# Mask loads and first-maxima loads begun by GpSimd, query loads spread over steps, and chains begun later, in a two-layer attention kernel

## The chip, the cores and the metric

The kernel runs on one core of a Trainium2 chip. The metric is the device time of one execution in microseconds. A core has five engines with a queue each: TensorE (PE in the profile; PEld are its weight loads), VectorE (DVE), ScalarE (ACT), GpSimd (POOL) and SyncE (SP), which only begins transfers here. An engine takes its instructions in the order of the program and waits at each for the semaphores that this instruction needs, so a waiting instruction holds all behind it.

## The reference

Two transformer layers work on x (2048 rows of 256) with 16 heads of 16.

```
layer 0: x0, x1 = halves of x (1024 rows each)
         each half: x += gate * self_attention(mod(ln(x)))
         xm, ym = mod(ln(x0)), mod(ln(x1));  x0 attends to ym, x1 attends to xm, gated
         x += gate * mlp(mod(ln(x)))          # 256 -> 1024 -> 256, gelu
layer 1: x = ln(x + attention(x, x, mask))    # scores = where(mask == 0, -1e9, scores)
         x = ln(x + attention(x, ctx))        # ctx: 1601 rows
         x = ln(x + mlp(x))                   # relu
attention: softmax(q k^T / 4) v, per head, then an output projection
```

The mask is a 2048 x 2048 array of int32. All is float32.

## The kernel before

**Stages, blocks, units, steps.** There are four attention stages: 0 self, 1 cross, 2 masked, 3 over the context. A stage goes over four blocks of 512 queries, a block over four groups of four heads. One group of one block is a unit. In stages 0 and 1 a unit has 16 steps, in stage 2 it has 32, in stage 3 it has 26. Block 2 of stage 2 goes first and is split into two parts by keys, so that its first part (4 units of 16 steps) needs only half the keys; the parts are joined at the end. This makes 1440 steps; one takes about 1.9 us.

**A step** does two things on TensorE. It makes one tile of scores of the current unit by key rows (L1160; in stage 2 the mask's bias is first added by L1153), adds the negated row maximum (L1167), takes the exponential on ScalarE (L1174), and adds an earlier tile's product with the values to the sums (L1191). And it makes one tile of scores of the *next* unit by query rows (L1079, and L1074 in stage 2), only for its maxima, which VectorE takes (L1089; in stage 2 L1082, which adds the bias by rows first). When a unit's maxima are complete they are negated and turned into a row tile `nm` (L1113, copied by ScalarE at L1118), three steps later. Both kinds of score tile share three PSUM buffers.

**Split block.** For its eight units the first maxima are needed in another layout too: `as_rows` begins eight small loads `mh<-nm` (L1125) and four steps later VectorE adds them (L1131, `minus`).

**End of a unit.** At step 2 of the next unit, `copy_sums` copies the sums (L1223) and moves them by 4 + 4 transfers (L1229, L1238) to `weights` and `oT`. Three steps later the weights are inverted and go through memory to `rd_rows` (L1260, L1262); six steps later GpSimd divides oT by them (L1269).

**Chains.** What follows attention for a block is a generator of the background: the projection (L544), a gate on GpSimd (`gated`, L563 and L565, which finish the tile `t`), normalization (statistics on VectorE, the power `rs` on GpSimd at L387, then L390), transposes (L405), in stages 1 and 3 the feed-forward layer (L602, L655; in stage 1 with a gate), then keys, queries (L454) and values (L490) of the next stage. Keys and queries are split into a high and a low part, `hi` (ScalarE, L467) and `lo` (VectorE, L468), in a ring of three buffers, and stored by SP (L472). Values go to a tile `v` that GpSimd first sets to one in part (L483). A chain is advanced by a step at a time, one piece of TensorE work each. `chain_after` sets when it may begin: 8 steps after `copy_sums`, or 9 for the split block.

**Order.** The program's order on every queue is what this planning writes out; nothing reorders it later. `later` holds actions with a countdown in steps; `after` runs those due, then one key or value transfer of the next stage, then advances the chain. A chain leaves out a step in which such an action, like the turn of nm, uses TensorE.

**Loads on SP.** `load_queries` (L981) begins the eight transfers of a unit's queries at step 1, two units ahead, into one of three buffers. `mask_rows` loads a 128 x 512 tile of the mask into one of two buffers `raw` (L1014), and GpSimd makes a bias tile of it (L1015). There are 64 such tiles: 8 for each part of the split block, one a step (`mask_part`), and 16 for each other block, begun among the maxima of the last unit of the block before. All transfers are begun by SP.

Of the kernel before, what the change touches and what calls it, by code (L numbers as in the profile page):

```python
# [12 lines left out]
F32 = mybir.dt.float32  # L13
# [9 lines left out]
P = 128  # L23
D = 256
H = 16
HD = 16
# [4 lines left out]
BLK = 512  # L31
# [45 lines left out]
def two_layers(ctx: ExitStack, tc: tile.TileContext, a: dict, out: bass.AP):  # L77
    nc = tc.nc
# [875 lines left out]
    def load_needed(kind, u):  # L954

        need = [(kind, u["st"], u["g"], slot) for slot in u["slots"]]
        load_ready(need)
        assert all(w in loaded for w in need)
# [11 lines left out]
        elif transfers:  # L970
            transfers.pop(0)[1]()

    def load_queries(u):
        st, b, g = u["st"], u["b"], u["g"]
        ensure(("q", st, b))
        u["q"] = sb.tile([P, 2, BLK], F32R, tag="q", bufs=3, name="q")
        d = queries_dr[st, b]
        for c in range(2):
            for i in range(4):
                at = 64 * c + HD * i  # L980
                nc.sync.dma_start(  # L981
                    u["q"][at : at + HD].bitcast(F32),
                    d[c, i // 2, 2 * g * HD : (2 * g + 2) * HD, :].rearrange(
                        "(q d) t -> d q t", d=HD
                    ),
                )

# [6 lines left out]
    def mask_rows(b, slot, qt, j):  # L996

        if (b, slot, qt) not in bias_rows:
            if b != SPLIT:
                t = sb.tile([P, 2, SLOT], BF16, tag="w_mlp", bufs=WB, name="bias")  # L1000
                for s in range(2):
                    bias_rows[b, s, qt] = t[:, s, :]
            elif slot == 0:

                t = sb.tile([P, TPB, SLOT], BF16, tag="kT11", name="bias")
                for q in range(TPB):
                    bias_rows[b, slot, q] = t[:, q, :]
            else:
                t = sb.tile([P, 2, SLOT], BF16, tag="w_mlp", bufs=WB, name="bias")
                for q2 in range(2):  # L1010
                    bias_rows[b, slot, qt + q2] = t[:, q2, :]
        raw = sb.tile([P, BLK], I32, tag="raw", bufs=2, name="raw")
        q0, k0 = b * BLK + qt * P, KEYS[2][slot][j] * BLK
        nc.sync.dma_start(raw, a["mask"][q0 : q0 + P, k0 : k0 + BLK])  # L1014
        nc.gpsimd.tensor_scalar(  # L1015
            bias_rows[b, slot, qt][:, j * BLK : (j + 1) * BLK], raw, 0.0, MASKED,
            ALU.is_equal, ALU.mult,
        )
# [26 lines left out]
    def maxima(u):  # L1045

        st, b, g = u["st"], u["b"], u["g"]
        masked = st == 2
        chunks = []
        for slot in u["slots"]:  # L1050
            nk = slot_rows(st, slot)
            n = -(-nk // BLK)
            size = -(-nk // n)
            size += size % 2
            nk += nk % 2
            chunks += [(slot, c, min(size, nk - c)) for c in range(0, nk, size)]

        def pair(qt, n, i):
            if "pm" not in u:
                load_needed("keys", u)  # L1060
                u["pm"] = sb.tile([P, TPB, 2, 2, len(chunks)], F32, tag="pm", bufs=2, name="pm")
            if masked and i == 0 and g == NG - 1 and 1 in u["slots"]:
                at = ORDER[2].index(b) + 1
                each = 2 * 2 // len(chunks)
                for j in range(n * each, (n + 1) * each) if at < NB else ():
                    mask_rows(ORDER[2][at], j // 2, qt, j % 2)
            slot, c, nn = chunks[n]
            s = big_ps()
            for h in range(2):
                queries = u["q"][64 * h : 64 * h + 64, i, qt * P : (qt + 1) * P]  # L1070
                keys = kT[g][slot][64 * h : 64 * h + 64, i, c : c + nn]
                if masked and h:
                    for part in range(2):
                        nc.tensor.matmul(  # L1074
                            exchanged(s[:, h, :], part), lhsT=queries,
                            rhs=exchanged(keys, 1 - part), start=True, stop=True,
                        )
                    continue
                nc.tensor.matmul(s[:, h, :nn], lhsT=queries, rhs=keys, start=True, stop=True)  # L1079
            if masked:  # L1080
                for h in range(2):
                    nc.vector.tensor_tensor_reduce(  # L1082
                        out=s[:, h, :], in0=s[:, h, :],
                        in1=bias_rows[b, slot, qt][:, c : c + nn],
                        scale=1.0, scalar=-3.0e38, op0=ALU.add, op1=ALU.max,
                        accum_out=u["pm"][:, qt, h, i, n : n + 1],
                    )
            else:
                nc.vector.tensor_reduce(u["pm"][:, qt, :, i, n], s[:, :, :nn], AX.X, ALU.max)  # L1089

        return [
            lambda qt=qt, n=n, i=i: pair(qt, n, i)
            for qt in range(TPB) for n in range(len(chunks)) for i in range(2)
        ]
# [14 lines left out]
    def as_rows(u):  # L1109

        m = one_ps()
        for qt in range(TPB):
            nc.tensor.matmul(  # L1113
                m[:, qt * P : (qt + 1) * P], lhsT=negpad[:, qt, :], rhs=identR,
                start=True, stop=True,
            )
        u["nm"] = sb.tile([P, BLK], F32R, tag="nm", bufs=2, name="nm")
        nc.scalar.copy(u["nm"], m)  # L1118
        if "part" in u:

            t = sb.tile([P, 2, 4 * BLK // P], F32, tag="mh", bufs=2, name="mh")
            for j in range(4):
                for h in range(2):
                    r = 64 * (j // 2) + 2 * (j % 2) + h
                    nc.sync.dma_start(  # L1125
                        t[PH * j : PH * (j + 1), h, :], u["nm"][r : r + 1, :].bitcast(F32)
                    )

            def add():
                n = u["minus"] = part_tile(u, "minus")  # L1130
                nc.vector.tensor_tensor(n, t[:, 0, :], t[:, 1, :], ALU.add)  # L1131

            later.append([4, add, False])
# [189 lines left out]
            nc.vector.reciprocal(rd[rows_, cut], rd[rows_, cut])  # L1323
            nc.vector.tensor_tensor(oT[:, cut], oT[:, cut], rd[rows_, cut], ALU.mult)

    def chain_after(u):

        go = now[0] + (9 if "part" in u else 8)

        def gen():  # L1330
            yield max(0, go - now[0])
            yield from chains[u["st"]](u["b"])

        background.append([gen(), 0, False])

    def stream(stages):
# [78 lines left out]
        streaming[0] = True  # L1415
        for u in units[:2]:
            load_queries(u)
        for step in range(math.floor(todo[-1][0]), 0):
            small[0] = 1
            evict()  # L1420
            take_maxima(step)
            after(step)
        pending: list = []
        step = 0
        for u in units:
            i = u["i"]
            masked = u["st"] == 2
            small[0] = i % 2
            second = weights_of(u)
            for s2 in range(len(second)):  # L1430
                if masked:
                    evict()
                if s2 == 3:
                    pending += values_of(u)
                if s2 == 1 and i + 2 < len(units):
                    load_queries(units[i + 2])

                if masked:
                    second[s2]()
                take_maxima(step)  # L1440
                f = pending.pop(0) if pending else None


                after(step)
                if f:
                    f()
                if not masked:

                    evict()
                    second[s2]()  # L1450
                step += 1
                if s2 == 2:
                    small[0] = (i + 1) % 2
                if s2 == 2 and i:
                    w = units[i - 1]
                    copy_sums(w)
                    part = w.get("part")
                    if part is None:
                        later.append([3, lambda w=w: invert(w), False])
                        later.append([6, lambda w=w: divide(w), False])  # L1460
                    elif part == 1:
                        v = units[i - 1 - NG]
                        later.append([3, lambda w=w, v=v: compare(w, v), False])
                        later.append([4, lambda w=w, v=v: invert_both(w, v), False])
                        later.append([7, lambda w=w: (fetch_first(w), divide(w)), False])
                    if w["g"] == NG - 1 and part != 0:
                        chain_after(w)
        small[0] = len(units) % 2
        last_t.append(residual(xs[3, units[-1]["b"]]))
        for f in pending:  # L1470
# [120 lines left out]
```

## Time and profile before

| | us |
|---|---|
| median of 3 runs | 3239.06 |
| the runs | 3213.37, 3239.06, 3241.68 |
| profiled execution, whole time | 3233.97 |
| its span in the trace | 3232.2 |
| TensorE busy | 2965.8 |
| VectorE busy | 2174.8 |
| ScalarE busy | 1718.1 |
| GpSimd busy | 389.5 |

The mean granted clock of TensorE is 0.97 of full. In the profile "A <- B" reads: A stood idle until B released it. "raw<-in_mask" names a transfer by what it writes and reads. In a timeline the columns are start, duration, engine, line, operation, tiles, shapes and count; a bracket tells the idle time before, and who ended it. In a table of windows each engine's busy time in the stretch is followed by its number of instructions; then come the granted clock, the share of time in which the DMA engines were busy, and GB/s.

By the trace, stage 0 and the unmasked part of stage 1 last until about 1199 us, the split block from 1199 to about 1640, the other masked blocks until about 2350, stage 3 to the end.

### The profile page before, as it was taken

Reading aid. Unit: us, or ns where it says so; the run is one execution under the profiler, and the core shown is the slowest. Engines: PE = TensorE matmul, PEld = TensorE weight load, DVE = VectorE, ACT = ScalarE, POOL = GpSimd, SP = SyncE. Lnnn points to the kernel's source line nnn. Section 1 sums busy time; section 2 is a strip of 40 time slices with the busy share of each in tenths; the row PEclk is TensorE's granted clock in tenths of the full one; section 3 lists DMA queues with packets and bytes.
Section 4 is the critical chain, followed back from the end, with each engine's and each line's share of the span. In section 5 each row is a group of like instructions: output and inputs, shape, how many; then the busy total and the mean of one; then the engine's idle time right before and its main releaser. Section 6 shows DMA issues by size and latency. Waiting matters only on the chain.

```text
span 3232.2 us, 60041 instructions
## 1 busy us (share of the span) xinstructions
PE 2965.8 (92%) x24128; PEld 1449.1 (45%) x24128; DVE 2174.8 (67%) x3945; ACT 1718.1 (53%) x1897; POOL 389.5 (12%) x333
## 2 busy tenths in 40 slices
PE   5899999999999889998999999999989999999997
PEld 2344444444444345444555555554444444444443
DVE  4676776767565647566878878877667757657452
ACT  1465655656464536443555555555556546546462
POOL 0001101101010121204013013110010110110110
PEclk8899999999999999998999999999999999999998
DMA  6462162162114321254111011003240000000000
GB/s 165 129 132 87 51 110 67 46 125 41 60 27 94 60 84 40 90 104 125 45 49 57 18 34 60 21 26 77 44 105 19 21 17 21 26 19 28 11 14 18
DMA packets 177155, 191.39 MB, mean 59 GB/s; under 512 B 94036, under 2 KB 110940, under 8 KB 176876
## 3 DMA queue, kind: packets, MB, share of 16 engines
q1 hardware_dynamic: 176876, 187.55, 23.6%
q8 instruction: 190, 3.11, 0.4%
q14 instruction: 89, 0.73, 0.1%
HBM read 129.78 MB, written 48.45 MB: 55 GB/s over the span
## 4 chain that ended last, share of the span: by engine, by line
PE 74%; DVE 7%; ACT 6%; DMA 6%; SPq 3%; issue 2%; POOL 1%; ACTq 0%; DVEq 0%; POOLq 0%
PE m_ps L1191 20%; PE s_ps L1160 16%; PE s_ps L1167 8%; PE s_ps L1079 7%; ACT e L1174 5%; PE s_ps L1153 5%; PE m_ps L602 3%; PE m_ps L655 3%; PE m_ps L454 2%; PE m_ps L490 2%; PE m_ps L544 2%; DVE s_ps L1082 2%; DMA kT<-k_dr 2%; DVE pm L1089 2%; PE s_ps L1074 2%
## 5 line engine op out<-in xcount | busy, mean ns | idle before, releaser
L1174 ACT ACTIVATE e<-s_ps 128x1024 f32<-128x1024 f32 (+1 forms) x1440 | 1466.4, 1024 | 1200.1 <-PE s_ps L1167 1180.8
L1089 DVE TENSOR_REDUCE pm<-s_ps 128x2 f32<-128x1024 f32 (+3 forms) x1024 | 1121.6, 1107 | 499.8 <-PE s_ps L1079 496.4
L1191 PE MATMUL m_ps<-e,V 128*32 128x256 f32 (+2 forms) x10432 | 910.6, 421 | 0.9 <-DVE lo L468 0.8
L1082 DVE CUSTOM_DVE_ANT_0 s_ps<-s_ps,bias 128x512 f32<-128x512 f32 x1024 | 712.7, 701 | 216.0 <-PE s_ps L1074 193.4
L1160 PE MATMUL s_ps<-q,kT 64*128 64x512 f32 (+1 forms) x2880 | 721.7, 498 | 28.8 <-ACT e L1174 23.3
L1079 PE MATMUL s_ps<-kT,q 64*128 64x512 f32 (+3 forms) x2560 | 602.0, 394 | 103.1 <-ACT e L1174 66.2
L1167 PE MATMUL s_ps<-nm,sel 64*128 64x512 f32 (+1 forms) x2880 | 574.2, 395 | 0.0
L1160 PEld LDWEIGHTS s_ps<-q,kT 64*128 64x128 f32 (+1 forms) x2880 | 270.0, 184 | 568.4 <-issue 404.4
L1079 PEld LDWEIGHTS s_ps<-kT,q 64*128 64x128 f32 x2560 | 293.1, 187 | 273.7 <-ACT e L1174 151.6
L1191 PEld LDWEIGHTS m_ps<-e,V 128*32 128x32 f32 (+1 forms) x10432 | 207.3, 109 | 348.5 <-issue 285.1
L1269 POOL TENSOR_TENSOR oT<-oT,rd_rows 64x512 f32<-64x512 f32 x63 | 80.2, 1273 | 1793.3 <-DMA rd_rows<-rd_dr 1419.8
L1167 PEld LDWEIGHTS s_ps<-nm,sel 64*128 64x128 f32 (+1 forms) x2880 | 276.1, 188 | 2.0
L1153 PE MATMUL s_ps<-biasT,ident 64*64 64x512 bf16 x2048 | 210.7, 402 | 9.0 <-DVE pm L1082 6.2
L1074 PE MATMUL s_ps<-kT,q 64*128 64x256 f32 x1024 | 206.0, 282 | 10.8 <-DMA kT<-k_dr 10.0
L1074 PEld LDWEIGHTS s_ps<-kT,q 64*128 64x128 f32 x1024 | 184.1, 185 | 33.6 <-issue 10.8
L1153 PEld LDWEIGHTS <-ident 64*64 64x64 bf16 x2048 | 58.3, 103 | 231.0 <-issue 164.4
L1015 POOL TENSOR_SCALAR bias<-raw 128x512 bf16<-128x512 int32 x64 | 123.6, 1931 | 247.8 <-DMA raw<-in_mask 233.0
L1082 DVE DVE_READ_ACCUMULATOR2_ANT pm<- 128x1 f32 x1024 | 144.8, 141 | 0.0
L454 PE MATMUL m_ps<-hT,w_qk 128*128 128x512 f32 (+2 forms) x224 | 111.9, 623 | 10.7 <-DVE lo L468 7.7
L602 PE MATMUL m_ps<-hT,w_mlp 128*128 128x512 f32 x224 | 111.1, 618 | 5.9 <-ACT sums L1223 4.4
L468 DVE SCALAR_TENSOR_TENSOR lo<-m_ps,qkb,hi 128x512 fp32r<-128x512 f32 (+3 forms) x60 | 42.0, 700 | 108.5 <-ACT hi L467 64.7
L655 PE MATMUL m_ps<-w_mlp,hid 128*128 128x256 f32 x448 | 105.0, 388 | 0.0
(118 smaller groups left out, 1414.9 us busy)
## 6 DMA issues: line engine op xcount, KB each, us to landing
q<-q_dr SPq DMA_DIRECT2D x544, 64.0 KB
kT<-k_dr SPq DMA_DIRECT2D x192, 128.0 KB
raw<-in_mask SPq DMA_DIRECT2D x64, 256.0 KB
q_dr<-hi SPq DMA_DIRECT2D x32, 256.0 KB
q_dr<-lo SPq DMA_DIRECT2D x32, 256.0 KB
oT<-sums SPq DMA_DIRECT2D x256, 32.0 KB
rd_rows<-rd_dr SPq DMA_DIRECT2D x63, 128.0 KB
k_dr<-hi SPq DMA_DIRECT2D x28, 256.0 KB
```

The source lines that it names most:

```text
L454: nc.tensor.matmul(m[:, :n], lhsT=wqk[:, k, w, c, :], rhs=hT[:, k, :n], start=k == 0, stop=k == 1)
L602: nc.tensor.matmul(m, lhsT=w1[k][:, f * P : (f + 1) * P], rhs=hT[:, k, :], start=k == 0, stop=k == 1,)
L655: nc.tensor.matmul(m[:, q2 * D : (q2 + 1) * D], lhsT=hid[f][:, qt * P : (qt + 1) * P], rhs=w2[f // 4][:, f % 4, :], start=f == 0, stop=f = ...
L1074: nc.tensor.matmul(exchanged(s[:, h, :], part), lhsT=queries, rhs=exchanged(keys, 1 - part), start=True, stop=True,)
L1079: nc.tensor.matmul(s[:, h, :nn], lhsT=queries, rhs=keys, start=True, stop=True)
L1082: nc.vector.tensor_tensor_reduce(out=s[:, h, :], in0=s[:, h, :], in1=bias_rows[b, slot, qt][:, c : c + nn], scale=1.0, scalar=-3.0e38, op0 ...
L1089: nc.vector.tensor_reduce(u["pm"][:, qt, :, i, n], s[:, :, :nn], AX.X, ALU.max)
L1153: nc.tensor.matmul(s[to : to + 64, h, :], lhsT=ident16[of : of + 64, of : of + 64], rhs=bias_columns[b, slot, kt][of : of + 64, :], start= ...
L1160: nc.tensor.matmul(s[:r, h, :], lhsT=kT[g][slot][64 * h : 64 * h + 64, i, kt * P : kt * P + r], rhs=u["q"][64 * h : 64 * h + 64, i, :], st ...
L1167: nc.tensor.matmul(s[:r, h, :], lhsT=sel[64 * h : 64 * h + 64, i, :r], rhs=u["nm"][64 * h : 64 * h + 64, :], start=False, stop=True,)
L1174: nc.scalar.activation(e[:r], s[:r], AF.Exp, scale=SCALE)
L1191: nc.tensor.matmul(u["av"][PH * j : PH * (j + 1), cut], lhsT=V[g][slot][:r, kt * GW + j * VW : kt * GW + j * VW + PH], rhs=u["e"][n, j % 2 ...
```

## The change

Four edits, in three parts.

1. `mask_rows` begins the load of raw on GpSimd's queue instead of SP's. In GpSimd's order each load then stands directly ahead of the instruction that makes the bias of it.
2. `as_rows` begins the eight loads mh on GpSimd's queue.
3. `load_queries` only allots the buffer and makes a list of eight loads. For the first two units all are issued at once; otherwise one is issued a step, and what is left is issued before the unit's maxima begin.
4. `chain_after` lets a chain begin 11 steps after `copy_sums` instead of 8, unless the current stage is the masked one. Together with the turn of nm at step 13 of a unit, the projection then stands at steps 14 and 15 of a 16-step unit (before: 10 and 11), in stage 3 at 13 and 14 (before: 10 and 11), and all that the chain does comes three or four steps later. In stage 2 the order on TensorE is the same as before.

```diff
-    def load_queries(u):
+    def load_queries(u, spread=False):
         st, b, g = u["st"], u["b"], u["g"]
         ensure(("q", st, b))
         u["q"] = sb.tile([P, 2, BLK], F32R, tag="q", bufs=3, name="q")
         d = queries_dr[st, b]
...
+        def load(c, i):
+            at = 64 * c + HD * i
+            nc.sync.dma_start(
+                u["q"][at : at + HD].bitcast(F32),
+                d[c, i // 2, 2 * g * HD : (2 * g + 2) * HD, :].rearrange("(q d) t -> d q t", d=HD),
+            )
+
+        u["loads"] = [lambda n=n: load(n // 4, n % 4) for n in range(8)]
+        if spread:
+            for n in range(8):
+                later.append([n, lambda: u["loads"] and u["loads"].pop(0)(), False])
...
-        nc.sync.dma_start(raw, a["mask"][q0 : q0 + P, k0 : k0 + BLK])
+        nc.gpsimd.dma_start(raw, a["mask"][q0 : q0 + P, k0 : k0 + BLK])
         nc.gpsimd.tensor_scalar(
             bias_rows[b, slot, qt][:, j * BLK : (j + 1) * BLK], raw, 0.0, MASKED,
...
             if "pm" not in u:
+                while u["loads"]:
+                    u["loads"].pop(0)()
                 load_needed("keys", u)
...
-                    nc.sync.dma_start(
+                    nc.gpsimd.dma_start(
                         t[PH * j : PH * (j + 1), h, :], u["nm"][r : r + 1, :].bitcast(F32)
                     )
...
-    def chain_after(u):
+    def chain_after(u, masked=False):
...
-        go = now[0] + (9 if "part" in u else 8)
+        go = now[0] + (9 if "part" in u else 8 if masked else 11)
...
             load_queries(u)
+            while u["loads"]:
+                u["loads"].pop(0)()
...
-                    load_queries(units[i + 2])
+                    load_queries(units[i + 2], spread=True)
...
-                        chain_after(w)
+                        chain_after(w, masked)
```

More of the change, by code (lines that the diff above doesn't have):

```diff
@@ L977, in load_queries @@
         d = queries_dr[st, b]
-        for c in range(2):
-            for i in range(4):
-                at = 64 * c + HD * i
-                nc.sync.dma_start(
[L982 to L986, printed above, removed]
+        def load(c, i):
[8 more added lines that the diff above has]
+                later.append([n, lambda: u["loads"] and u["loads"].pop(0)(), False])
     bias_rows: dict = {}
@@ L1124, in as_rows @@
                     r = 64 * (j // 2) + 2 * (j % 2) + h
-                    nc.sync.dma_start(
+                    nc.gpsimd.dma_start(
                         t[PH * j : PH * (j + 1), h, :], u["nm"][r : r + 1, :].bitcast(F32)
```

## The prediction

> **What bounds the kernel now.** I read the page's busy shares and clock row first, then the waits, then the stretches where TensorE (PE) idles, then the queues there.
>
> ```profile
> PE 2965.8 (92%) x24128; PEld 1449.1 (45%) x24128; DVE 2174.8 (67%) x3945; ACT 1718.1 (53%) x1897; POOL 389.5 (12%) x333
> PEclk8899999999999999998999999999999999999998
> ```
>
> PE is busy 92%, 2966 of 3232 us. Only the other 266 us, and what a lowered clock costs, can be won by moving transfers. The windows show that little of it is general:
>
> ```profile
> 1050.00:1100.00 50.00, 38.02 (x286) 17.81 (x279) 29.50 (x40) 23.50 (x26) 7.35 (x6) 0.93 0.55 92
> 1150.00:1200.00 50.00, 37.87 (x240) 19.53 (x239) 22.30 (x37) 18.12 (x22) 19.45 (x12) 0.86 0.34 112
> 1350.00:1400.00 50.00, 40.67 (x327) 19.44 (x319) 25.12 (x68) 18.90 (x21) 0.00 (x0) 0.90 0.54 101
> 1500.00:1550.00 50.00, 39.45 (x290) 20.38 (x288) 30.08 (x88) 16.54 (x21) 23.97 (x14) 0.86 0.34 109
> 1700.00:1750.00 50.00, 50.00 (x512) 25.51 (x513) 41.59 (x113) 28.97 (x30) 4.63 (x3) 1.00 0.11 31
> ```
>
> The columns are PE, PEld, DVE, ACT, POOL busy, then the granted clock. The steady masked stage (1700) has no hole. Around the start of that stage single holes of 6 to 11 us stand, and each drags the clock down: 0.86 over 50 us is 7 us of full clock, beside 11.2 us of standing. PE's waits name them:
>
> ```profile
> PE m_ps L490 <- DVE lo L468: 28.9, 8, 11.2
> PE m_ps L544 <- POOL oT L1269: 11.8, 3, 6.1
> PE s_ps L1074 <- DMA kT<-k_dr: 10.0, 2, 7.8
> PE m_ps L405 <- ACT sums L1223: 10.0, 7, 1.4
> PE m_ps L454 <- DVE lo L468: 7.7, 14, 1.7
> ```
>
> (total, times, longest). The longest L490 wait is explained by SP's queue at that moment:
>
> ```profile
> 1161.96 7.59 SPq L1014 DMA_DIRECT2D raw<-in_mask  x4
> ...
> 1173.09 0.38 SPq L472 DMA_DIRECT2D k_dr<-hi  x1
> ```
>
> Four mask loads, each waiting until GpSimd (POOL) has used up one of two raw buffers, stand ahead of the store of hi. DVE waits 11.9 us for that store to free its tile, and PE waits for DVE.
>
> **What is won.** (1) With raw off SP, that 11.2 us stall goes. (2) The 7.8 us wait for keys at 1375: SP held the last three key loads behind eight mh loads (issued 1365.48 to 1370.5, after a wait for nm). Without them the loads go some 5 us earlier; I leave 1.5 us, so 6.3. (3) Projections start at step 14 of a unit, not step 10 (11 instead of 8, and the turn of nm at step 13 pushes them on): four steps of 1.9 us (64 steps lie between the projections at 249.3 and 371.6) outlast L544's waits of 1.5, 6.1 and 4.2, so 11.8. (4) The same shift takes four 1.4 us waits of L405 behind ACT's sums away, 5.7 us, and lets hi and lo be stored after the weights and oT copies of step 2 are issued (389.60 to 395.8 on SP): 5 of L454's 7.7 us. The shift's loads of x and its residual go with it and were never waited for. Its PE work is the same rows, 0. Long stalls: 29.3; short ones: 10.7.
>
> The stalls at 1484 and 1531 (3.1 and 7.4 us, again L490 behind lo) have the same cause as (1), but I don't count them: there POOL becomes late instead, below.
>
> **What it costs.** 64 mask loads and 64 mh loads (first maxima) move onto POOL: in its order each raw load now stands directly ahead of its own bias (L1015), so load and use cannot overlap any more. Before, SP ran ahead by two buffers:
>
> ```profile
> 1321.49 1.92 POOL L1015 TENSOR_SCALAR bias<-raw 128x512 bf16<-128x512 int32 x1 [0.97 <-DMA raw<-in_mask]
> 1323.49 1.27 POOL L563 TENSOR_TENSOR u<-u,rows 128x512 f32<-128x512 f32 x1
> 1324.84 1.27 POOL L565 TENSOR_TENSOR t<-t,u 128x512 f32<-128x512 f32 x1
> 1326.19 3.92 POOL L1015 TENSOR_SCALAR bias<-raw 128x512 bf16<-128x512 int32 x2
> ```
>
> No POOL-issued DMA is in this trace. A mask tile takes at least what SP's took from issue to use, 1161.96 to 1165.27 or 3.3 us, plus 1.92 for the bias: 5.2. The Trainium skill ("DMA: Bandwidth & Descriptors", Anatomy of one DMA) fits a GpSimd-issued DMA with 2.0 us plus its bytes at 436 GB/s: 2.6 for 256 KB, so 4.5 a tile. I bound it by 5.0 and 6.5 (3.3 + 1.1 of POOL's own time + 1.92 + 0.2) and take 5.4, by the row. An mh load is bounded by SP's 0.6 (eight in 4.94 us) and 1.1 (POOL's smallest operation, rs 128x4, takes 1.02); I take 0.9. Neither can gain POOL anything, since POOL issued none before.
>
> One rule speaks against the change: "SBUF — State Buffer", Who interferes with whom, says DVE in its two-port modes locks GpSimd out while it writes descriptors, and the page measured 620 ns becoming 3100. By it a tile costs 5.4 + 2.5 = 7.9. But the DVE rows between 1490 and 1512 are almost all L1082, with scores from PSUM and one SBUF operand; by the same section such an instruction does not contend. I stay with 5.4 and keep 7.9 as a case.
>
> In most of the kernel POOL is 12% busy and this hides: in a full masked block 16 tiles take 86 us, used one to two units (62 us each) later. If that cover were gone, L1082 would stand for the difference. Four places lack it. They are counted on the trace's times; in the first, the step times once the feed-forward matmuls stand four steps later. A waiting mh also holds what follows it on POOL: rs, tiles, gates and divides.
>
> - *First masks* (from about 1137, when the last reader of their tile ends): the gate L563/L565 of block 0, now four steps later, comes behind four tiles. L565 ends at 1166, PE wants its transposes at 1164: 2. Four more tiles and a divide precede the memset of v, done 1189, wanted 1184: 5.
> - *rs at 1264.66* is behind eight mh: 1261.1 + 7.2 + 1.0 = 1269.3 against L390 at 1265.93: 3.5.
> - *Gate of block 1*: nm is ready at 1308.5, then eight mh (7.2), five tiles (27.0) and two L563/L565 pairs (5.2): 1347.9. PE takes t at 1335.0 (L405): 12.9 us. Behind POOL's queue stand x_dr's store on SP and all of PE.
> - *Second part, 1452 to 1554*: eight mh from 1452.1 to 1459.3; four tiles to 1480.9; divide and first-part sums, limited by rd_rows until 1483.5, to 1487.4; two tiles, 1498.2; eight mh, 1505.4; ten tiles, 1559.4; eight mh, 1566.6; landing 2.0: 1568.6. DVE reads that mh at L1131 at 1553.5, and all later maxima are queued behind it: 15.1 us, the two stalls there already inside the old times.
>
> Sum of stalls: 7 + 3.5 + 12.9 + 15.1 = 38.5 against 29.3 won: +9.2. For the clock I add 0.35 us per us of long stall (7 us beside 11.2 is 0.6; half of it, as PE waits for DVE for part of it): 9.2 x 1.35 = +12.4. Less 10.7 of short waits: +2 us on the profiled execution's 3234.0 (span 3232.2 plus 1.8): 3236 us. That execution is 5 us under the median of the three runs, 3239.1; I don't correct for it.
>
> **Queries one transfer a step.** 66 units load eight transfers; issue is 8 x 0.45 us either way, none on PE's path. The last goes at step 8 or 9 and is forced before its maxima at step 12 of 16: three steps, 5.6 us, against 2.2 us for a landing (chain of waits at 386). Cost 0; with keys reloading (eight q issued in 7.6 us at 705) the cover is thin.
>
> **Rivals.**
>
> A, *faster*: POOL's issue is cheap, tile 5.0 and mh 0.6. The places become 4.7 + 1.0 + 8.5 + 5.5 = 19.7 (same sums), so (19.7 - 29.3) x 1.35 - 10.7 = -24: 3210 us. For it: POOL's low share, the page's 2.6 us. Against: a serial tile can't be under 5.
>
> B, *slower*: POOL's order takes the place of SP's as the late one, tile 6.5 and mh 1.1. First masks 13, rs 5.3, gate 20.0, second part 34.9: 73.2, so (73.2 - 29.3) x 1.35 - 10.7 = +49: 3283 us. The deciding point is the mh of the last unit against L1131 at 1553.5: from a tile time of about 6.1 on (mh at 1.1: 30 us there, 63 in all) the sum is over 1% slower. With the lock-out, tile 7.9 (mh 0.9): 22, 3.5, 25.4 and 52.5, so +89: 3323.
>
> C, *spread queries land late*: in the 16 units that reload keys PE stands 2 us each, x 1.35 = 43 on top of the forecast: 3279. Against it: a forced load still precedes the maxima and only 16.9 us in two waits, at the start, are due to q now.
>
> **Numbers.** No change (within 1%, 32 us, about what a measurement of this kernel can tell: its own runs spread over 28 us) 0.38, A 0.32, B with the lock-out 0.25, C 0.05. Forecast 3236; range 3200 to 3290, leaving out the lock-out's end and gains beyond A. Faster 0.32, same 0.38, slower 0.30.
>
> **What would show it.** Right: no PE wait on lo over 3 us at 1150 to 1200; L544's waits on oT gone; raw and mh issued by POOL, every bias waiting for its raw load with 5 to 6 us between biases; new PE waits for POOL's t near 1340 and DVE waits at the sum of mh near 1555. Wrong: bias ops 4.5 us apart or less, or no wait at L1131 (then A); PE waits on q (then C); POOL's issues over 1.2 us (then B).

## The result, and the profile after

The changed kernel takes 3321.65 us, the median of four runs (3318.39 to 3322.56), against 3238.82 us for four runs of the kernel before: a ratio of 1.0275, 95% interval 1.0253 to 1.0297. It is 83 us slower, where no change was forecast. The profiled execution took 3318.39 us, its span 3316.6.

Read first what answers to the first lines of the prediction, from the page of the changed kernel:

```profile
PE 2999.7 (90%) x24128; PEld 1464.4 (44%) x24128; DVE 2185.0 (66%) x3945; ACT 1720.2 (52%) x1897; POOL 458.8 (14%) x461
PEclk8889999998999999999899999999999999999998
```

PE runs the same 24128 matmuls, but for 34 us longer: the granted clock is 0.953 over the span, 0.970 before. The other 50 us are idle time. The windows of the changed kernel (columns as in the prediction) say where:

```profile
200.00:250.00 50.00, 34.43 (x256) 14.28 (x256) 24.52 (x26) 20.69 (x22) 2.51 (x2) 0.85 0.59 99
1700.00:1750.00 50.00, 49.95 (x510) 26.71 (x504) 39.37 (x110) 31.32 (x39) 4.09 (x4) 1.00 0.13 31
```

The masked stage at 1700 is as full as it was. Stage 0 at 200 is not; the kernel before had this in the same stretch:

```profile
200.00:250.00 50.00, 44.67 (x385) 19.66 (x384) 36.41 (x35) 31.69 (x34) 3.84 (x3) 1.00 0.65 113
```

A third of the matmuls is missing there, and the clock has gone from 1.00 to 0.85. By the starts of the exponentials in the traces, one for each step, step 512 (the end of stages 0 and 1) comes at 1228 us before and 1314 after, step 1024 (the end of stage 2) at 2349 and 2449: 86 us are lost in stages 0 and 1, 13 in stage 2, and stage 3 gives 15 back.

PE's waits in the changed kernel (total us, times, longest):

```profile
PE s_ps L1085 <- DMA q<-q_dr: 74.7, 19, 16.2
...
PE s_ps L1085 <- DMA kT<-k_dr: 13.4, 2, 9.6
PE m_ps L405 <- DMA c<-in_ctx: 11.7, 2, 11.0
PE s_ps L1085 <- issue: 10.3, 2, 7.6
...
PE m_ps L405 <- POOL t L565: 8.9, 2, 7.2
...
PE m_ps L490 <- DVE lo L468: 4.3, 4, 3.0
PE m_ps L544 <- POOL oT L1275: 4.2, 1, 4.2
```

(L1085 is L1079 of the kernel before, L1275 is L1269.) The two waits that were to go, on lo and on oT, have gone from 40.7 us to 8.5. In their place PE stands at L1085, the first matmul of a unit's maxima, for queries; the lines that name kT and "issue" are the same wait, since PE goes on within 0.3 us of the landing of a query load there too. Of the 98.4 us, 17.2 are two waits at the start, which were there before (16.9 us). That leaves 81 us in 21 waits, all before step 512.

The case in which SP was latest is seen on PE in the changed kernel near 210 us (start, duration, engine, line, work, and in brackets the idle time before):

```profile
206.53 0.39 PE L1085 MATMUL s_ps<-kT,q 64*128 64x512 f32 x1
213.76 0.76 PE L1085 MATMUL s_ps<-kT,q 64*128 64x512 f32 x1 [6.84 <-DMA q<-q_dr]
```

and its cause in SP's queue of the changed kernel ahead of it:

```profile
185.52 0.42 SPq L981 DMA_DIRECT2D q<-q_dr  x1
185.99 0.42 SPq L913 DMA_DIRECT2D kT<-k_dr  x1
190.81 2.52 SPq L1235 DMA_DIRECT2D weights<-sums  x4
193.37 2.99 SPq L1244 DMA_DIRECT2D oT<-sums  x4
196.40 0.58 SPq L981 DMA_DIRECT2D q<-q_dr  x1
...
199.87 0.37 SPq L1266 DMA_DIRECT2D rd_dr<-rd  x1
203.11 0.59 SPq L1268 DMA_DIRECT2D rd_rows<-rd_dr  x1
203.75 0.45 SPq L913 DMA_DIRECT2D kT<-k_dr  x1
204.24 0.41 SPq L981 DMA_DIRECT2D q<-q_dr  x1
...
206.96 0.43 SPq L201 DMA_DIRECT2D rows<-in_rows  x1
209.11 0.94 SPq L207 DMA_DIRECT2D rows<-mod_dr  x2
210.09 0.43 SPq L981 DMA_DIRECT2D q<-q_dr  x1
```

An SP issue of 0.42 us costs nothing; what counts is where the queue has gaps. SP waits from 186.4 to 190.8 for ScalarE's sums, from 200.2 to 203.1 for rd_dr to land, and from 207.4 to 209.1 for the landing of rd_rows, begun at 203.11:

```profile
SPq L207 <- DMA rd_rows<-rd_dr: 1.7, 1, 1.7
```

This last wait has nothing to do with the row that is loaded there. SP's transfers in this program use eight semaphores in turn, and rd_rows is the transfer eight places before the row's. The eighth query load of the unit stands behind all three. It is begun at 210.09, when PE has already been standing since 206.9. In the kernel before, the same loads stood ahead of all of them:

```profile
177.31 5.39 SPq L981 DMA_DIRECT2D q<-q_dr  x8
182.75 0.89 SPq L913 DMA_DIRECT2D kT<-k_dr  x2
183.73 3.47 SPq L1229 DMA_DIRECT2D weights<-sums  x4
...
191.38 0.37 SPq L1260 DMA_DIRECT2D rd_dr<-rd  x1
195.13 0.59 SPq L1262 DMA_DIRECT2D rd_rows<-rd_dr  x1
```

There they filled SP's time before the sums.

The place in SP's queue is only part of it: a late load also took longer to land. In another unit SP began the last load in time, and PE stood just as long:

```profile
520.27 0.42 SPq L981 DMA_DIRECT2D q<-q_dr  x1
527.74 0.79 PE L1085 MATMUL s_ps<-kT,q 64*128 64x512 f32 x1 [6.84 <-DMA q<-q_dr]
```

PE stopped at 520.90, and the load begun at 520.27 landed 7.4 us after its issue. From 515 to 528 the DMA engines were 0.87 busy, with keys among other things; whether that is the reason isn't shown. The 21 waits lie in 20 of the last 30 units of stages 0 and 1. In these 20 the last load was begun 0.9 us before PE stopped (mean; in five of them after it), and PE went on 5.0 us after that issue. In the kernel before, the last load of these 30 units was begun 24.6 us ahead of its maxima and landed 2.3 us after its issue (means).

### The profile page after: what moved, and what is told of

Read it like the earlier page. It is cut to its first block, busy times and chain, and to the rows that moved or that the text cites. A ratio compares the mean times of both kernels' runs of the same rounds, so it can differ in the third digit from the quotient of the medians.

```text
span 3316.6 us, 60040 instructions
## 1 busy us (share of the span) xinstructions
PE 2999.7 (90%) x24128; PEld 1464.4 (44%) x24128; DVE 2185.0 (66%) x3945; ACT 1720.2 (52%) x1897; POOL 458.8 (14%) x461
## 4 chain that ended last, share of the span: by engine, by line
PE 45%; DVE 5%; ACT 3%; issue 2%; POOL 2%; DMA 2%; SPq 1%; ACTq 0%; POOLq 0%; DVEq 0%
PE m_ps L1197 13%; PE s_ps L1166 10%; PE s_ps L1173 5%; PE s_ps L1159 4%; PE s_ps L1085 4%; ACT e L1180 2%; PE m_ps L602 2%; DVE s_ps L1088 2%; DVE pm L1095 1%; PE s_ps L1080 1%; PE m_ps L655 1%; PE m_ps L544 1%; POOL bias L1019 1%; PE m_ps L454 1%; DMA raw<-in_mask 1%
## 5 line engine op out<-in xcount | busy, mean ns | idle before, releaser
L1180 ACT ACTIVATE e<-s_ps 128x1024 f32<-128x1024 f32 (+1 forms) x1440 | 1467.3, 1024 | 1272.1 <-PE s_ps L1173 1263.1
L1095 DVE TENSOR_REDUCE pm<-s_ps 128x2 f32<-128x1024 f32 (+3 forms) x1024 | 1122.4, 1107 | 601.0 <-PE s_ps L1085 598.1
L1085 PE MATMUL s_ps<-kT,q 64*128 64x512 f32 (+3 forms) x2560 | 615.6, 398 | 176.4 <-DMA q<-q_dr 74.7
L1166 PE MATMUL s_ps<-q,kT 64*128 64x512 f32 (+1 forms) x2880 | 726.5, 501 | 22.3 <-ACT e L1180 13.8
L1173 PE MATMUL s_ps<-nm,sel 64*128 64x512 f32 (+1 forms) x2880 | 579.2, 398 | 0.0
L1085 PEld LDWEIGHTS s_ps<-kT,q 64*128 64x128 f32 x2560 | 297.9, 190 | 354.2 <-ACT e L1180 148.7
L1275 POOL TENSOR_TENSOR oT<-oT,rd_rows 64x512 f32<-64x512 f32 x63 | 80.4, 1277 | 1718.2 <-DMA q<-q_dr 947.8
L1173 PEld LDWEIGHTS s_ps<-nm,sel 64*128 64x128 f32 (+1 forms) x2880 | 278.9, 190 | 2.4
L655 PE MATMUL m_ps<-w_mlp,hid 128*128 128x256 f32 x448 | 111.4, 405 | 9.6 <-ACT sums L1229 9.6
L655 PEld LDWEIGHTS m_ps<-w_mlp,hid 128*128 128x128 f32 x448 | 87.9, 201 | 30.4 <-ACT sums L1229 10.5
```

Source lines behind the costliest of these rows:

```text
L655: nc.tensor.matmul(m[:, q2 * D : (q2 + 1) * D], lhsT=hid[f][:, qt * P : (qt + 1) * P], rhs=w2[f // 4][:, f % 4, :], start=f == 0, stop=f = ...
L1166: nc.tensor.matmul(s[:r, h, :], lhsT=kT[g][slot][64 * h : 64 * h + 64, i, kt * P : kt * P + r], rhs=u["q"][64 * h : 64 * h + 64, i, :], st ...
L1173: nc.tensor.matmul(s[:r, h, :], lhsT=sel[64 * h : 64 * h + 64, i, :r], rhs=u["nm"][64 * h : 64 * h + 64, :], start=False, stop=True,)
L1180: nc.scalar.activation(e[:r], s[:r], AF.Exp, scale=SCALE)
```

## Experiments

Each run is set against the kernel before on the same chip, whose medians beside them lay between 3228.1 and 3232.3 us. Differences between two versions are taken from the ratios (0.001 is 3.2 us), since not all ran side by side.

| label | queries | chain | raw | mh | us | ratio (95%) |
|---|---|---|---|---|---|---|
| spread_only | one a step | 8 | SP | SP | 3374.0 | 1.0447 (1.0415 to 1.0480) |
| pool_only | at once | 8 | GpSimd | GpSimd | 3250.6 | 1.0077 (1.0053 to 1.0102) |
| chain_only | at once | 11 | SP | SP | 3210.7 | 0.9949 (0.9930 to 0.9969) |
| burst | at once | 11 | GpSimd | GpSimd | 3225.3 | 0.9990 (0.9976 to 1.0003) |
| q_act | one a step, on ScalarE | 11 | GpSimd | GpSimd | 3317.7 | 1.0268 (1.0253 to 1.0284) |
| rows_pool | one a step, rd pair on GpSimd | 11 | GpSimd | GpSimd | 3272.6 | 1.0133 (1.0103 to 1.0163) |
| late_burst | at once, behind the copies | 11 | GpSimd | GpSimd | 3213.9 | 0.9941 (0.9926 to 0.9957) |
| spread2 | two a step | 11 | GpSimd | GpSimd | 3203.8 | 0.9913 (0.9898 to 0.9928) |
| chain_raw | at once | 11 | GpSimd | SP | 3223.0 | 0.9971 (0.9958 to 0.9984) |
| chain_mh | at once | 11 | SP | GpSimd | 3197.8 | 0.9891 (0.9864 to 0.9919) |
| two_chain | two a step | 11 | SP | SP | 3190.5 | 0.9879 (0.9857 to 0.9901) |
| two_ahead | two a step | 11 | GpSimd, one ahead | GpSimd | 3171.8 | 0.9822 (0.9800 to 0.9845) |
| burst_inv4 | at once, inversion a step later | 11 | GpSimd | GpSimd | 3205.8 | 0.9926 (0.9902 to 0.9949) |

**Which part is it?** The changed kernel with the queries loaded as before:

```diff
-                    load_queries(units[i + 2], spread=True)
+                    load_queries(units[i + 2])
+                    while units[i + 2]["loads"]:
+                        units[i + 2]["loads"].pop(0)()
```

> The changed kernel, but all eight query loads of a unit issued at once, at step 1, as before. Theory Q (the spread query loads come late behind SP's waits, and this is all of the loss): 3220 to 3240 us, PE's waits on q back to about 17 us, all at the start. Rival P (GpSimd's serial order of loads, biases and gates is the loss): 3300 or more. Rival K (the later chain moves its loads and stores against the key loads): also 3300 or more.

It took 3225.3 us: the whole loss is gone, and of PE's waits on q these are left, the same as before the change:

```profile
PE s_ps L1085 <- DMA q<-q_dr: 16.7, 2, 15.6
```

Its step 512 comes at 1213 us, against 1314 with the spread, so 102 us arise by then. Of these, 64 us are more idle time of PE: the 81 us of waits, less 17 us of other waits that became shorter. The other 38 us are longer matmuls, at a granted clock of 0.922 instead of 0.961. The reverse, the kernel before with the spread alone:

```diff
-                    load_queries(units[i + 2])
+                    load_queries(units[i + 2], spread=True)
```

> The kernel before, with the query loads spread and nothing else. Theory Q: 3310 to 3340 us, PE's waits on q near 75 us in all. Rivals P and K: within 1% of before, 3210 to 3270. If the spread only hurts together with the later chain, which puts more on SP at the same steps: between, about 3270.

It took 3374.0 us, 34 us above the upper end of what was expected. Its waits show a second victim:

```profile
PE s_ps L1085 <- DMA q<-q_dr: 67.5, 12, 15.6
...
PE m_ps L544 <- POOL oT L1275: 40.8, 11, 7.8
...
PE s_ps L1085 <- issue: 27.4, 5, 8.7
```

The rd pair now also comes later: counted from the first exponential of the unit, rd_rows is begun 1.2 us later than before and GpSimd's division 1.4 us later (medians in stages 0 and 1). So oT is late for a projection that begins 8 steps behind the sums (40.8 us, 11.8 before). With the chain at 11 steps that wait is 4.2 us. So the later chain softens what the spread does. The two other parts alone:

```diff
-        nc.sync.dma_start(raw, a["mask"][q0 : q0 + P, k0 : k0 + BLK])
+        nc.gpsimd.dma_start(raw, a["mask"][q0 : q0 + P, k0 : k0 + BLK])
...
-                    nc.sync.dma_start(
+                    nc.gpsimd.dma_start(
                         t[PH * j : PH * (j + 1), h, :], u["nm"][r : r + 1, :].bitcast(F32)
```

> The kernel before, with raw and mh begun by GpSimd and nothing else. By the sum on record at the measured tile of 4.95 us and mh of 0.5 us: about 10 to 15 us less than before, 3220 to 3235. Rival P: 3280 or more.

```diff
-        go = now[0] + (9 if "part" in u else 8)
+        go = now[0] + (9 if "part" in u else 8 if masked else 11)
```

> The kernel before, with chains begun 11 steps behind the sums where steps have no mask, and nothing else. By steps 3 and 4 on record, without what GpSimd's new order would cost: 15 to 25 us less than before, 3210 to 3225. Rival K: 3260 or more.

GpSimd's part alone costs 25 us (3250.6), so neither the sum's 3220 to 3235 nor the rival's 3280 was met. The chain alone gains 16 us (3210.7), inside its range.

**Why are the loads late: the queue, or the step?** The same loads at the same steps, begun by ScalarE:

```diff
-            nc.sync.dma_start(
+            nc.scalar.dma_start(
                 u["q"][at : at + HD].bitcast(F32),
```

> The changed kernel with the query loads begun by ScalarE's queue instead of SP's, at the same steps, one a step. Theory Q1 (the loads are late because of what stands ahead of them in SP's order): PE's waits on q fall back to about 17 us and the time to 3220 to 3260 us; the upper end if 0.45 us of ScalarE for each of 512 issues delays exponentials. Rival S (one a step is too late a place, or single transfers are slower, in whatever queue): 3300 or more, with waits on q near 75 us.

The waits on q fall to the 16.6 us at the start, so neither the step nor single transfers make them late. Over the same 30 units the last load is now begun 11.8 us ahead of its maxima and lands in 2.9 us; on SP, at the same step, it was 4.7 and 4.3 us (means). The time doesn't fall (3317.7): another cost of the same size came in. PE's waits of this kernel:

```profile
PE s_ps L1085 <- DVE pm L1095: 66.1, 79, 2.7
...
PE s_ps L1166 <- DVE pm L1095: 32.2, 50, 4.3
PE s_ps L1085 <- DMA q<-q_dr: 16.6, 2, 13.5
```

and ScalarE's:

```profile
ACT e L1180 <- DMA q<-q_dr: 95.2, 103, 1.3
```

PE's waits on the maxima L1095 rise from 24.3 us in burst to 98.3, and the loss is in all stages (76 us behind burst at step 1024). The last line looks like exponentials held up by the query loads, but it is not: each of these 103 exponentials starts 0.1 us after the last matmul of its own scores (L1173), like those whose wait is put down to L1173, and the loads named had been begun some 1.9 us before and landed at about that moment. So the exponentials waited for scores as always. How loads in ScalarE's queue make the maxima late, no run shows.

All eight loads at once, but behind the copies of the sums:

```diff
-                later.append([n, lambda: u["loads"] and u["loads"].pop(0)(), False])
+                later.append([2, lambda: u["loads"] and u["loads"].pop(0)(), False])
```

> The changed kernel with all eight query loads at once, but two steps later than before, directly behind the eight copies of the sums. Theory Q1: eight issues of 0.45 us behind the copies go out by 200 us in the unit whose maxima begin at 206, so no waits on q: 3225 to 3245 us. If standing behind the copies is itself enough to be late: 3270 or more.

```profile
187.81 2.95 SPq L1244 DMA_DIRECT2D oT<-sums  x4
190.85 3.79 SPq L981 DMA_DIRECT2D q<-q_dr  x8
...
196.14 0.37 SPq L1266 DMA_DIRECT2D rd_dr<-rd  x1
```

SP in this kernel: one wait ahead of the loads, and they are out by 194.6. 3213.9 us, 11 us under the range expected. Standing behind one waiting instruction is not late here. Two loads a step, the last pair three steps after the first:

```diff
-                later.append([n, lambda: u["loads"] and u["loads"].pop(0)(), False])
+                later.append([n // 2, lambda: u["loads"] and u["loads"].pop(0)(), False])
```

> The changed kernel with two query loads a step, so that the last goes four steps after the first and ahead of the stores and loads of the inverted sums. Theory Q1: those stores and loads are what the late ones stand behind, so most of the loss goes: 3225 to 3260 us. If every load behind the copies of the sums comes late: still 3280 or more. Rival S: about half of the loss, 3270.

3203.8 us, 3.6% or 117 us below the changed kernel and 21 below the range expected, for a pace of two instead of one. And one a step on SP, with the rd pair taken off SP:

```diff
-        nc.sync.dma_start(d.rearrange("j (p c) -> (j p) c", p=PH), rd)
+        nc.gpsimd.dma_start(d.rearrange("j (p c) -> (j p) c", p=PH), rd)
...
-        nc.sync.dma_start(dst[at : at + P // 2, :], d.unsqueeze(1).to_broadcast([4, HD, BLK]))
+        nc.gpsimd.dma_start(dst[at : at + P // 2, :], d.unsqueeze(1).to_broadcast([4, HD, BLK]))
```

> The changed kernel, one query load a step on SP, but rd_dr and rd_rows begun by GpSimd, directly ahead of the product there that waits for rd_rows anyway. Theory Q1: it is these two that the late query loads stand behind on SP; without them waits on q fall to 20 to 30 us in all and the time to 3200 to 3240 us. Rival S (one load a step is too late a place by itself, or the copies of the sums are enough): 3290 or more, with waits on q near 60 to 75 us.

3272.6 us, above the range of theory Q1 and under rival S's. By step 512, 43 of the 102 us are left, and of the 81 us of waits 45 (q and "issue", 61.8 us together, less 17.3 at the start). The time also has a new wait of 20.7 us at 1553, for a maximum: there mh stands behind the rd pair in GpSimd's queue. SP's queue in this kernel near 210 us, and one of its waits there:

```profile
202.59 0.91 SPq L207 DMA_DIRECT2D rows<-mod_dr  x2
207.41 0.33 SPq L201 DMA_DIRECT2D rows<-in_rows  x1
...
209.84 0.43 SPq L981 DMA_DIRECT2D q<-q_dr  x1
SPq L201 <- DMA kT<-k_dr: 3.9, 1, 3.9
```

With the rd pair gone, SP comes to the chain's row loads earlier and waits there until 207.4, for the landing of the key transfer eight places before. The eighth load leaves at 209.84, nearly as late as before. But this is one of only two units where PE stopped first. In the other eight that still wait, the last load was begun 0.5 to 6.1 us before PE stopped and PE went on 6.1 to 9.5 us after its issue. So theory Q1 was half right: the rd pair held the loads, and other waits of SP take its place in part, but most of what is left here is slow landing. That part of rival S, that a load at these steps on SP comes too late even when the queue lets it through, stands.

**What GpSimd's part costs.** mh or raw alone on GpSimd, with the later chain:

```diff
-                    nc.gpsimd.dma_start(
+                    nc.sync.dma_start(
                         t[PH * j : PH * (j + 1), h, :], u["nm"][r : r + 1, :].bitcast(F32)
```

> Chains 11 steps behind the sums and raw begun by GpSimd; mh stays with SP and queries are loaded at once. Theory M (what GpSimd costs is mh standing behind a run of mask tiles, which holds VectorE at the sum of mh): no wait at the sum of mh, and the time is that of the later chain alone or less, 3200 to 3215 us. Rival T (the mask tiles themselves come late, or hold gates and powers): 3220 to 3230, like the version with both.

```diff
-        nc.gpsimd.dma_start(raw, a["mask"][q0 : q0 + P, k0 : k0 + BLK])
+        nc.sync.dma_start(raw, a["mask"][q0 : q0 + P, k0 : k0 + BLK])
```

> Chains 11 steps behind the sums and mh begun by GpSimd; raw stays with SP and queries are loaded at once. By step 2 on record, 6.3 us x 1.35 less than the later chain alone: about 3203 us. If mh on GpSimd stands behind biases that wait for raw: 3211 to 3220, with VectorE waiting at the sum of mh.

(Both diffs are from burst.) mh on GpSimd gains 19 us on chain_only (3197.8), raw on GpSimd loses 7 (3223.0). Theory M in its first form fell: mh on SP is in time, VectorE has no wait for it, but chain_raw has PE waiting 24.2 us for c and lies in rival T's range. The path is seen best in burst, where PE waits 20.1 us for c. GpSimd does there

```profile
1536.78 0.58 POOL L1018 DMA_DIRECT2D raw<-in_mask  x1
1539.74 1.93 POOL L1019 TENSOR_SCALAR bias<-raw 128x512 bf16<-128x512 int32 x1 [2.38 <-DMA raw<-in_mask]
1541.73 0.21 POOL L483 MEMSET v<- 128x64 f32 x1
1541.82 3.98 POOL L1131 DMA_DIRECT2D mh<-nm  x8
```

and SP

```profile
1541.97 0.31 SPq L525 DMA_DIRECT2D v_dr<-v  x1
1542.71 0.33 SPq L773 DMA_DIRECT2D c<-in_ctx  x1
```

A run of mask tiles, 4.95 us each and more, ends at 1541.7. Only then comes the memset that the tile v needs; the store of v has stood at the head of SP's queue since 1518.0 for it, and the load of c stands behind that store on SP. In burst mh comes behind it too, and VectorE stands 22.05 us at the sum of mh. If the length of the run is the cause, a shorter run cures both:

```diff
-        nc.gpsimd.tensor_scalar(
+        later.append([0, lambda: nc.gpsimd.tensor_scalar(
             bias_rows[b, slot, qt][:, j * BLK : (j + 1) * BLK], raw, 0.0, MASKED,
             ALU.is_equal, ALU.mult,
-        )
+        ), False])
```

> The changed kernel with two query loads a step, and each bias one step behind its raw load, so that GpSimd has the next raw load under way while it makes a bias: a tile should take about 2.6 us of GpSimd instead of 4.95. Theory M (what GpSimd costs is the length of its serial run of mask tiles before the sum of mh, and the store of v behind it): the wait for c near step 622 goes and the time is 3185 to 3195 us. Rival: as with two loads a step alone, 3204.

```profile
1498.40 1.13 POOL L1018 DMA_DIRECT2D raw<-in_mask  x2
1501.56 3.93 POOL L1019 TENSOR_SCALAR bias<-raw 128x512 bf16<-128x512 int32 x2 [2.02 <-DMA raw<-in_mask]
1505.55 0.21 POOL L483 MEMSET v<- 128x64 f32 x1
1505.64 4.01 POOL L1131 DMA_DIRECT2D mh<-nm  x8
```

In the split block two loads are now under way together, and a tile takes 3.6 us (1498.40 to 1505.55 for two), not the 2.6 hoped for. The 48 tiles of the other blocks still go one by one, some 4.9 us each. The shorter runs of the split block are enough: the waits for c are down to 1.0 us, those for the gate's t are gone, VectorE's longest wait for mh is 3.6 us, and the kernel takes 3171.8 us. This is 13 us under the range expected, 29 less than with two loads a step alone and the fastest of all, 1.8% under the kernel before and 4.4% under the changed one. Without GpSimd's part, two loads a step add to the later chain as forecast:

```diff
-                later.append([n, lambda: u["loads"] and u["loads"].pop(0)(), False])
+                later.append([n // 2, lambda: u["loads"] and u["loads"].pop(0)(), False])
...
-        nc.gpsimd.dma_start(raw, a["mask"][q0 : q0 + P, k0 : k0 + BLK])
+        nc.sync.dma_start(raw, a["mask"][q0 : q0 + P, k0 : k0 + BLK])
...
-                    nc.gpsimd.dma_start(
+                    nc.sync.dma_start(
```

> Chains 11 steps behind the sums and two query loads a step; raw and mh stay with SP. If the parts add: 21 us less than the later chain alone with its loads at once (the step from 3225 to 3204), so about 3190 us. If the query loads now stand behind mask loads that wait for GpSimd: as the later chain alone, 3210, or more.

3190.5 us, 23 below the later chain alone. GpSimd's part in its best form is worth 18 us on top of that (two_ahead), no more than mh alone gained on chain_only (19). So no run shows a gain from moving raw; two loads a step with mh on GpSimd and raw left on SP was not run.

**A gain that nobody had foreseen.** spread2 and late_burst are 25 and 16 us faster than burst, with no fewer waits on q. Burst again, with the inversion and the division of the sums one step later:

```diff
-                        later.append([3, lambda w=w: invert(w), False])
-                        later.append([6, lambda w=w: divide(w), False])
+                        later.append([4, lambda w=w: invert(w), False])
+                        later.append([7, lambda w=w: divide(w), False])
```

> The changed kernel with the queries loaded at once, and the inversion of the sums with its two transfers, and the division, one step later. With loads at once PE waits about 0.4 and 1.0 us at the ninth and tenth step of most units, 25 us in stages 0 and 1 and 13 in stage 3; in every version with query loads behind the copies, which also sends these two transfers out later, the waits of stage 3 are gone. Theory R (the time of these two transfers makes the waits): they are gone here too and the time is 3200 to 3210 us. Rival: the waits stay and the time is 3220 to 3230.

3205.8 us, 21 below burst. PE's waits on exponentials at the ninth and tenth steps of stage 3 fall from 13.8 us in burst to 2.8; those of stages 0 and 1 (25.4 us) have moved to the tenth and eleventh steps and are 19.8. So they follow the inversion and division of the sums. Query loads between the copies and the inversion push that later in time, and there too the waits of stage 3 are 2.8 us. How a transfer or a division on another engine makes PE wait for an exponential, no run shows.

## Why the prediction was wrong, step by step

- **Queries one transfer a step: the step that failed.** It said that "the last goes at step 8 or 9 and is forced before its maxima at step 12 of 16: three steps, 5.6 us, against 2.2 us for a landing ... Cost 0". Both terms were wrong. The three steps are the order in which the program is written, and SP is not in step with it: near 210 us it stood 2.9 us for rd_dr and 1.7 for an earlier transfer between two loads of one unit. In the 20 units that wait, 0.9 us are left of the 5.6. And the 2.2 us held for the loads at their old place (2.3 there); here it is 5.0 us from the last issue until PE goes on. The rule that a moved step must be followed past each instruction of its new queue was applied to raw and mh, and not here, though the eight issues in 7.6 us at 705 that it quotes were already SP waiting for its own landings. The cost is 93 us (spans of the changed kernel and burst, 3316.6 and 3224.0).
- **Rival C** had the mechanism and gave it 0.05. Its size was 2 us in each of 16 units; there are 21 waits of 3.9 us on average, in 20 units. Its argument against, that a forced load precedes the maxima, is true of the program's order and not of the time of the transfer.
- **The sum without the queries held, in part by luck.** It gave +2 us; burst, which is just that, measured -2.8 (interval -7.7 to +1.0). Two errors cancel in it. The chain (steps 3 and 4) was to gain 11.8 x 1.35 + 10.7 = 27 and gained 16: three waits of 3.2 us behind ACT's sums, at L655, came in place of those at L405, which the step didn't look for. GpSimd's part, less what steps 1 and 2 win, was to cost (38.5 - 17.5) x 1.35 = 28 and cost 13 (burst against chain_only; 25 with the chain at 8 steps).
- **Step 1** was right: waits of L490 on lo 28.9 to 4.3 us. (Of the four mask loads in the row that it reads, only the last two waited for GpSimd, and a wait for rd_dr stood ahead of the store too.) **Step 2** was right in kind: the wait for keys is 0.9 us in the changed kernel, and mh on GpSimd alone gains 19 us, where 6.3 x 1.35 = 8.5 was forecast. **Step 3**: 11.8 to 4.2, as the wait at the first projection of stage 3 stayed.
- **What it costs: the tile.** 5.4 us was taken, bounds 5.0 to 6.5; measured 4.95 where nothing else comes between (0.59 to issue, 2.36 of waiting, 1.93 for the bias, 0.07 between), just under the lower bound. mh is 0.5 us against 0.9, bounds 0.6 to 1.1. The bounds came from SP's row (3.3 us from issue to use), and there the Trainium skill did better: "DMA: Bandwidth & Descriptors", Anatomy of one DMA, gave 2.6 us for the load; issue to landing is 2.9. The lock-out of "SBUF — State Buffer", Who interferes with whom, would have made it 7.9 (an estimate) by a longer issue; the longest of the 64 issues took 0.78 us, so none is seen.
- **The places.** First masks: 1.6 us of PE waiting for t, forecast 7; rs: no wait of PE, forecast 3.5 (rival B's 5.3 there should be 5.0 by its own numbers). Gate of block 1: 7.2 us, forecast 12.9 and by rival A's numbers 8.5. Second part: forecast 15.1 us at the sum of mh; VectorE stands 13.8 us there (18.2 with an earlier one), and what reaches PE is 11.0 us at another instruction, L405 for c. The forecast saw VectorE behind mh, but not SP behind the memset of v, which is in the same run and is enough by itself (24.2 us in chain_raw).
- **The clock.** 0.35 us per us of stall was taken. From burst to the changed kernel, up to step 512, PE is busy 38 us longer beside 64 us more idle time: 0.6, the figure that the prediction had read off its one stall before it halved it.

## What to carry to other kernels

A transfer's place in the program is not its time: before a load is moved to a later step, walk its queue from the old place to the new one and add up what every instruction on the way waits for, because the load inherits all of it. Add the time to land as it is at the new place: it was 2.3 us at the old one and about twice that at the new one. Loads with long slack belong ahead of the queue's waiting instructions, or directly behind the first one, and not strewn among them. An issue that comes late in program order may also wait for earlier transfers of its own queue to land. Where load and use of a buffer are on one in-order engine, put the next load ahead of the present use, or each tile pays the latency.

## What the hardware showed that was not expected

- Which engine begins a transfer mattered far more than the time to begin it. The Trainium skill ("DMA: Bandwidth & Descriptors", Issuing engines are not separate DMA queues) says that beginning transfers on several engines only saves sequencer time, which is usually small. Here one issue is 0.42 us, and moving the 544 of them from SP to ScalarE took 81 us of PE's waits away: what was saved is not issue time but what stood ahead in SP's order. (The time of the kernel did not fall, since PE's waits on the maxima grew.)
- SP waits for its own transfers. In all 89 places of the changed kernel where SP is seen to wait for an earlier transfer on the semaphore that its next one uses, that is the transfer eight places before, 52.6 us in all. In those places SP had eight transfers under way and stood until the oldest had landed.
- The 64 KB query loads landed 2.3 us after issue where they were begun ahead of the copies (last of each unit, kernel before) and 4.3 us at the changed kernel's steps on SP, the longest 7.7.
- GpSimd begins a 256 KB load of the mask in 0.59 us and eight mh loads in 4.0 us, beside a busy VectorE; the longest of the 64 mask issues took 0.78 us.
